# Selective scans in tiles of four states by 32 channels instead of two states by 64, with dt passed on through device memory

## The chip, the core and the metric

The kernel runs on one core of a Trainium2 chip. The metric is the time of one execution on the device, in microseconds (us), as the median of several runs. A profile is one further execution, recorded by the hardware profiler; its span is the time from the first to the last instruction.

The engines: TensorE (PE) multiplies matrices, VectorE (DVE) works elementwise and runs scans, ScalarE (ACT) evaluates functions, GpSimd (POOL) works elementwise, SyncE (SP) issues the DMA transfers. Each executes its own instructions in the order in which they were put into the program; semaphores tie the engines together.

## What is computed

The input is 4 images of 384 channels by 32 x 32 positions, all in fp32. Two layers follow each other, each with a sequence mixer and a feed-forward part. Cut to what matters:

```python
# both mixers: a selective scan over t = 0..1023, 16 states n for each channel d
h[d, n] = h[d, n] * exp(dt[d, t] * A[d, n]) + (dt[d, t] * u[d, t]) * B[n, t]
y[d, t] = sum over n of h[d, n] * C[n, t]

# layer 0: four directions k, 384 channels, each with its own weights
xd = x_proj[k] @ xs[k]                     # rows dt (12), B (16), C (16)
dt = softplus(dt_proj[k] @ xd[:12] + bias)
y  = sum over k of (scan + D * u), turned back; layer norm; gelu
# layer 1: 768 channels, one direction
xin, z = in_proj(x); u = silu(conv4(xin)); scan with dt, B, C from u
out = layernorm(out_proj((y + D * u) * silu(z)))
# after layer 0: a feed-forward of Kronecker weights; after layer 1: 4 experts, best 2
```

## The kernel before

Two functions follow each other: `conv_layers` (L219), which holds all of layer 0 and the mixer of layer 1, and `moe_layer` (L1086), the experts. The change is in the first alone.

**The passes.** A pass (L756 to L778) is one image, one direction or one half of the 768 channels, and one half of the 1024 positions: 384 channels by 512 positions by 16 states. Layer 0 has 8 passes for an image, layer 1 has 4, so there are 48. The order of images and layers is fixed (`order`, L756): layer 1 of an image lies between the layer-0 passes of others.

**The steps.** A pass has 16 steps of three tiles each; a tile is 128 x 512, and its partitions hold two states of 64 channels. A step does:

- `load` (L845): SP fetches the step's B rows (`bt`) and C rows (`ct`) from device memory and broadcasts each to 64 partitions, two transfers for each of the two. Both have rings of three buffers.
- `times_b` (L854): POOL multiplies `dtus` (dt times u) by B for three tiles at once, into a slot of `s`, a ring of five.
- `decay` (L857): ACT computes exp(dt times A) from `dts` into `da`, one PSUM bank for each tile of a step.
- `scan` (L863): DVE runs the recurrence along the 512 positions. A first pass starts from 0, a later one from `state`; `keep_state` (L877) copies the last column.
- `times_c` (L901) and `times_c_pool` (L910): the result times C, by DVE for the first tiles of a step (the scan has then written to `da`) and by POOL for the rest (the scan has written to `s`). `share[i]` says how many DVE takes.
- `add` (L885): PE multiplies each tile by `both`, 128 x 64 of zeros and ones, which sums the two states into 64 partitions of `acc`, three PSUM banks for 384 channels. The tiles of a step go to the halves of PE's columns in turn.
- `gather` (L897, L466, L677): once in a pass, DVE adds `acc` and the D term into the layer's result.

**Ahead of a pass** (`prep_pass`, L374): PE multiplies by the dt weights (L381), ACT adds the bias (L390) and takes softplus (L393, which needs another function table: `exp_set` at L239 loads the old one back), POOL multiplies by u (L397), and SP copies dt and dt times u from SBUF to SBUF into `dts` and `dtus`, which hold each channel once for each of the two states (L409). `prep_quad0` and `prep_quad1` (L436, L645) make the rows of B and C.

**The rest** is side work: layer norms (L312), the feed-forward (`post0`, L482), projection and convolution of layer 1 (`prep1`, L593), gate and output projection (`post1`, L684). It shares all engines with the scans, two PSUM banks (`ps`), three buffers `tmp`, six `t1` and four `w`.

**The order of the work.** A planner (`Plan`, L117) writes out each engine's instructions before anything runs. The steps' instructions are `Op`s (L108) in streams, with a cost and what they depend on; side work is generators (`Lane`, L90), which yield an engine and a cost before each instruction. `run` (L181) takes, over and over, the instruction that can start first by its own clock, and `choose` (L1009) decides between a step's instruction and side work: on ACT side work goes if the next decay is not late by the plan or if it has waited 6 us (`AGE`), on POOL `pool_choice` (L979) does the like, and `split` (L1001) sets `share` by how far POOL is ahead. A DMA counts as 0.1 us on SP in this clock, whatever it is. Side jobs of the images follow each other in one chain (L816): the input of an image's layer 1 is ready only when the chain has reached it. On the chip each engine follows the written order, and waits where something is later than planned.

## Time and profile before

| | |
|---|---|
| median of 3 runs | 6737.26 us (6733.55 to 6745.8) |
| the profiled execution's own time | 6755.91 us |
| its span | 6754.0 us |
| first scan | at 68.86 us |
| last gather of the scans | at 4474 us, then 2.06 us |
| scans stand still | from 4030 to about 4113 us |
| experts | from about 4600 us to the end |
| busy in the span: PE, DVE, ACT, POOL | 5601.9, 4145.4, 2735.4, 4080.2 us |
| mean granted clock of PE | 0.883 |

A line of a group in the profile gives the line of the code, engine and operation, what is written and read, shapes and count; then the busy time in us and the mean of one in ns; then the idle time of the engine just before these instructions, with what ended it. An fp32 matmul of this kernel has two records, so 2304 sums show as 4608. Durations of neighbours overlap a little in the records (two products C of 0.68 us end 1.27 us after the first began), so the pace of an engine is read from start to start. PE's time contains pipelined work and is no measure of its peak. An instruction on a DMA queue (SPq) lasts for as long as it holds the queue; when its data has landed is given apart. Idle time of an engine costs nothing unless another waits for it.

### The profile page before, as it was taken

How to read it: one execution, taken by the hardware profiler on the slowest of the kernel's cores; microseconds unless marked ns; L12 is line 12 of the kernel's file. 1: busy time of each engine (PE TensorE's matmuls, PEld its weight loads, DVE VectorE, ACT ScalarE, POOL GpSimd, SP SyncE). 2: the span in 40 equal slices, each digit the busy share in tenths (PEclk: the TensorE clock that was granted, in tenths of full speed). 3: DMA queues.
4: the chain of work that ended last, by engine and by line, in shares of the span. 5: the costliest groups of instructions: out<-in, count | busy, mean ns of one | idle time of the engine just before them, and what ended most of it. 6: DMA issues, size and time to landing. Idle time of an engine off the chain costs nothing. (4 is left out here: it accounts for less than half of the span.)

```text
span 6754.0 us, 47474 instructions
## 1 busy us (share of the span) xinstructions
PE 5601.9 (83%) x12352; PEld 1929.1 (29%) x12352; DVE 4145.4 (61%) x5421; ACT 2735.4 (41%) x3911; POOL 4080.2 (60%) x1735
## 2 busy tenths in 40 slices
PE   6666789767777876878886897767899999999999
PEld 1111123112122211222221222223444444444444
DVE  6999989998889999899999885951100000000000
ACT  4444565555455645555555554432211111111111
POOL 6999888998889888999899875950000000000000
PEclk8787889887888988888887888888999999999999
DMA  4444444444445444445444433422000000000000
GB/s 130 143 140 143 138 119 141 143 134 124 133 139 159 136 132 139 130 144 157 144 142 138 118 109 106 148 88 105 0 0 0 28 0 8 21 0 0 10 14 14
DMA packets 413489, 644.55 MB, mean 95 GB/s; under 512 B 75104, under 2 KB 119200, under 8 KB 413216
## 3 DMA queue, kind: packets, MB, share of 16 engines
q1 hardware_dynamic: 413216, 641.52, 31.6%
q8 instruction: 97, 1.59, 0.1%
q14 instruction: 176, 1.44, 0.1%
HBM read 468.77 MB, written 21.50 MB: 73 GB/s over the span
## 5 line engine op out<-in xcount | busy, mean ns | idle before, releaser
L855 POOL TENSOR_TENSOR s<-dtus,bt 128x1536 f32<-128x1536 f32 x768 | 2640.6, 3447 | 177.6 <-PE acc L889 94.6
L889 PE MATMUL acc<-s,both 128*64 128x512 f32 x4608 | 2030.3, 742 | 838.1 <-POOL s L913 547.2
L861 ACT ACTIVATE da<-dts,a 128x512 f32<-128x512 f32 x2304 | 1511.2, 683 | 1469.2 <-DVE s L902 1305.7
L1226 POOL TENSOR_TENSOR xb<-xb,yg 128x1536 f32<-128x1536 f32 x32 | 118.8, 3712 | 1834.3 <-DVE yg L1223 1775.4
L1223 DVE SCALAR_TENSOR_TENSOR yg<-py,pvt,gate 128x512 f32<-128x512 f32 x96 | 66.2, 746 | 1848.8 <-PE py L1200 1846.6
L913 POOL TENSOR_TENSOR s<-s,ct 128x512 f32<-128x512 f32 (+1 forms) x673 | 1044.8, 1554 | 207.6 <-DVE state L883 54.4
L889 PEld LDWEIGHTS acc<-s,both 128*64 128x64 f32 x4608 | 483.7, 156 | 2323.9 <-POOL s L913 985.7
L1200 PE MATMUL py<-hid,w 128*128 128x512 f32 x2304 | 1046.2, 592 | 1.5 <-DVE yg L1223 1.5
L1212 PE MATMUL ph<-tb,w 128*128 128x512 f32 x2304 | 1046.3, 592 | 0.0
L870 DVE TENSOR_TENSOR_SCAN da<-da,s 128x512 f32<-128x512 f32 x736 | 871.4, 1219 | 169.3 <-POOL s L855 101.0
L870 DVE TENSOR_TENSOR_SCAN da<-da,state,s 128x512 f32<-128x512 f32 x720 | 889.3, 1273 | 100.0 <-ACT da L861 90.3
L902 DVE TENSOR_TENSOR s<-da,ct 128x512 f32<-128x512 f32 x1456 | 944.0, 682 | 10.9 <-DMA ct<-rows 6.2
L1216 ACT ACTIVATE hid<-ph,pvt 128x512 f32<-128x512 f32 x384 | 263.9, 687 | 1523.2 <-PE ph L1212 1516.9
L1200 PEld LDWEIGHTS py<-hid,w 128*128 128x128 f32 x2304 | 437.7, 190 | 553.9 <-issue 550.4
L1212 PEld LDWEIGHTS ph<-tb,w 128*128 128x128 f32 x2304 | 438.0, 190 | 552.2 <-issue 551.9
L870 DVE TENSOR_TENSOR_SCAN s<-da,state,s 128x512 f32<-128x512 f32 x432 | 550.4, 1274 | 15.8 <-ACT da L861 15.8
L870 DVE TENSOR_TENSOR_SCAN s<-da,s 128x512 f32<-128x512 f32 x416 | 503.8, 1211 | 18.1 <-ACT da L861 17.9
L591 PE MATMUL ps<-u,w 128*128 128x512 f32 x576 | 294.8, 660 | 35.9 <-DMA w<-in_w_in_dram 29.0
L381 PE MATMUL ps<-xd,dtw 12*128 12x512 f32 (+1 forms) x288 | 188.8, 749 | 32.7 <-ACT dt L390 24.5
L543 PE MATMUL ps<-t,w 32*128 32x512 f32 x192 | 148.4, 904 | 40.8 <-DMA w<-in_w_fc_dram 38.6
L591 PEld LDWEIGHTS ps<-u,w 128*128 128x128 f32 x576 | 114.9, 209 | 219.1 <-issue 171.9
L724 PE MATMUL ps<-yx,w 128*128 128x512 f32 x288 | 144.6, 655 | 38.9 <-DMA w<-in_w_out_dram 36.4
(134 smaller groups left out, 3278.1 us busy)
## 6 DMA issues: line engine op xcount, KB each, us to landing
bt<-rows SPq DMA_DIRECT2D x1536, 128.0 KB, 3.0
ct<-rows SPq DMA_DIRECT2D x1536, 128.0 KB, 3.0
dts<-dt SPq DMA_DIRECT2D x192, 256.0 KB, 3.9
dtus<-dt SPq DMA_DIRECT2D x192, 256.0 KB, 3.4
dts<-dt SPq DMA_DIRECT2D x192, 128.0 KB, 3.2
dtus<-dt SPq DMA_DIRECT2D x192, 128.0 KB, 3.5
w<-in_w_dram SPq DMA_DIRECT2D x8, 2304.0 KB, 23.9
w<-in_w_in_dram SPq DMA_DIRECT2D x48, 192.0 KB, 3.0
```

Of the source, the lines that this page charges most:

```text
L381: nc.tensor.matmul(pd, lhsT=q["dtw"][QROW : QROW + nr, c * P : (c + 1) * P], rhs=q["xd"][QROW : QROW + nr, cols(h)], start=True, stop=True,)
L543: nc.tensor.matmul(ph[h], lhsT=w[:32, j, :], rhs=z[h][:32], start=True, stop=True)
L591: nc.tensor.matmul(pi, lhsT=w[:, c, :], rhs=u[:, c, cols(h)], start=c == 0, stop=c == NC - 1)
L855: nc.gpsimd.tensor_tensor(ss[i % NSR], dtus[place(i)[1]], rep(bts[i % NBR]), ALU.mult)
L861: nc.scalar.activation(das[x], dts[part][:, x, :], AF.Exp, scale=q["a"][:, g, m : m + 1])
L870: nc.vector.tensor_tensor_scan(d if in_psum else s, d, s, 0.0 if first else state[:, j, x : x + 1], ALU.mult, ALU.add)
L889: nc.tensor.matmul(acc[side * HP : (side + 1) * HP, c, :], lhsT=both, rhs=ss[i % NSR][:, x, :], start=m == 0, stop=m == NS // 2 - 1,)
L902: nc.vector.tensor_tensor(ss[i % NSR][:, x, :], das[x], cts[i % NCR], ALU.mult)
L913: nc.gpsimd.tensor_tensor(s[:, m:, :], s[:, m:, :], rep(cts[i % NCR], NC - m), ALU.mult)
L1200: nc.tensor.matmul(py[:, m, :], lhsT=w2[:, f, m * P : (m + 1) * P], rhs=hid, start=f == 0, stop=f == NF - 1,)
L1212: nc.tensor.matmul(ph, lhsT=w1[:, c, f * P : (f + 1) * P], rhs=ts[i][:, c, :], start=c == 0, stop=c == NC - 1)
L1216: nc.scalar.activation(hid, ph, AF.Gelu, bias=pv("b1", e * NF + f))
```

## The change

A tile's partitions hold four states of 32 channels instead of two of 64, and a step has four tiles (`NG`) instead of three; a pass has 12 steps, and a chunk of four steps covers 128 channels with all 16 states. Following from it:

- B and C rows are broadcast to 32 partitions each, four transfers for each of `bt` and `ct` in a step.
- POOL's product with B covers four tiles; `share` is 3 by default, and POOL takes none, one or two tiles of a step's product with C.
- `da` has four PSUM banks; the tiles of a step are summed by `four`, 128 x 32, into the four quarters of the partitions of one bank, `acc`. All four sums are one entry of the plan.
- `acc` holds 128 channels, so it is gathered at each chunk's end, 144 times in place of 48, and a chunk's first sum waits for the gather before it.
- dt and dt times u are made in two buffers `tmp`, written to device memory (`spread`), and read from there into `dts` and `dtus`, 128 channels at a time, four transfers for each. These have two buffers in turn of chunks; the next load into one waits for the last decay, or the last product with B, of the chunk two before.
- `s` has four slots of four tiles; `ps` has three banks; `tmp` has four buffers, of which the preparation of a pass claims two.
- The dt weights and projected rows lie in one tile each, in two halves that take turns; layer 1 loads its dt weights once for an image.
- The planner remembers when a buffer was given back (`Free.clock`), and a lane's next instruction isn't planned ahead of that time (`floor`). Its costs and places in a step (`STEP`, `C`, `AT`) are those of steps of four tiles, `SPARE` is 3.6 instead of 6.0, and on PE sums take precedence when they are more than one step behind instead of two.

The diff, cut to its core:

```diff
+        yield "at", at
+        return tile
 
     def give(self, *tiles):
-        self.tiles.extend(tiles)
+        self.tiles.extend((Free.clock, t) for t in tiles)
 
 
...
+        self.floor = now
         try:
             self.want = next(self.gen) if sent is None else self.gen.send(sent)
+            while self.want is not None and self.want[0] == "at":
+                self.floor = max(self.floor, self.want[1])
+                self.want = next(self.gen)
         except StopIteration:
             self.done = True
 
     def ready(self):
-        return self.want[2] if len(self.want) > 2 else self.end
+        return max(self.want[2] if len(self.want) > 2 else self.end, self.floor)
 
 
...
-    dt, dtu = tiles(2, [P, NC, T], "dt")
-    dts = tiles(2, [P, NC, T], "dts")
-    dtus = tiles(2, [P, NC, T], "dtus")
-    xds = tiles(2, [64, L], "xd")
-    dtws = tiles(2, [64, D], "dtw")
+    NG, NJ = 4, 4 * NC
+    dts = tiles(2, [P, NG, T], "dts")
+    dtus = tiles(2, [P, NG, T], "dtus")
+    xd = sp.tile([P, L], F32, name="xd")
+    dtw = sp.tile([P, 2 * D], F32, name="dtw")
     wxs = tiles(2, [P, NC, QROW + R0], "wx")
-    NSR, NBR, NCR = 5, 3, 3
-    ss = tiles(NSR, [P, NC, T], "s")
+    NSR, NBR, NCR = 4, 3, 3
+    ss = tiles(NSR, [P, NG, T], "s")
     bts = tiles(NBR, [P, T], "bt")
     cts = tiles(NCR, [P, T], "ct")
-    state = sp.tile([P, NS, NC], F32, name="state")
-    tmp = Free(tiles(3, [P, NC, T], "tmp"))
+    state = sp.tile([P, NJ, NG], F32, name="state")
+    tmp = Free(tiles(4, [P, NC, T], "tmp"))
     t1 = Free(tiles(6, [P, T], "t1"))
     wts = Free(tiles(4, [P, NC, P], "w"))
-    acc = ps_1.tile([P, NC, T], F32, name="acc")
-    das = tiles(NC, [P, T], "da", pool=ps_1)
-    ps = Free(tiles(2, [P, T], "ps", pool=ps_1))
+    acc = ps_1.tile([P, T], F32, name="acc")
+    das = tiles(NG, [P, T], "da", pool=ps_1)
+    ps = Free(tiles(3, [P, T], "ps", pool=ps_1))
...
     nc.vector.tensor_tensor(spread, spread, proj2[:32, :D], ALU.mult)
 
 
-    both = wp.tile([P, HP], F32, name="both")
-    nc.vector.tensor_tensor(both, ident[:, :HP], ident[:, HP:], ALU.add)
-    a0 = wp.tile([P, 8 * NC, NS // 2], F32, name="a0")
-    a1 = wp.tile([P, 2 * NI, NS // 2], F32, name="a1")
+    four = wp.tile([P, QP], F32, name="four")
+    nc.vector.tensor_tensor(four, ident[:, :QP], ident[:, QP : 2 * QP], ALU.add)
+    for k in (2, 3):
+        nc.vector.tensor_tensor(four, four, ident[:, k * QP : (k + 1) * QP], ALU.add)
+    a0 = wp.tile([P, 4 * NC * NG, NS // 4], F32, name="a0")
...
     def prep_pass(q, p, h, u, u_view):
 
 
...
+        spread = dram.tile([2, D, T], F32, tag="dts", name="dts", bufs=3)
+        dt = yield from tmp.take(True)
+        dtu = yield from tmp.take(True)
         for c in range(NC):
             pd = yield from ps.take(True)
             yield PE, 0.95
             nc.tensor.matmul(
                 pd,
-                lhsT=q["dtw"][QROW : QROW + nr, c * P : (c + 1) * P],
-                rhs=q["xd"][QROW : QROW + nr, cols(h)],
+                lhsT=dtw[dt_rows(q), q["w0"] + c * P : q["w0"] + (c + 1) * P],
+                rhs=xd[dt_rows(q), cols(h)],
                 start=True,
                 stop=True,
             )
...
         yield ACT, 1.45 + SWITCH
         nc.scalar.activation(dt, dt, AF.Softplus)
         exp_set()
+        yield SP, LOAD
+        nc.sync.dma_start(out=spread[0].rearrange("(c p) t -> p c t", p=P), in_=dt)
         for c in range(NC):
             yield POOL, 1.35
             nc.gpsimd.tensor_tensor(u_view(dtu[:, c, :]), u_view(dt[:, c, :]), u[:, c], ALU.mult)
-        for part in range(2):
-            before = 0.0
-            if p:
-                before = yield from until(("scan", NS * (p - 1) + 8 * part + 7, 2))
-            for to, of in ((dts[part], dt), (dtus[part], dtu)):
-                yield SP, LOAD, before
-                for side in range(2):
-                    mine = [x for x in range(NC) if (3 * part + x) % 2 == side]
-                    chunks = [(3 * part + x) // 2 for x in mine]
-                    for k in range(2):
-                        nc.sync.dma_start(
-                            out=to[k * HP : (k + 1) * HP, mine[0] : mine[-1] + 1 : 2, :],
-                            in_=of[side * HP : (side + 1) * HP, chunks[0] : chunks[-1] + 1, :],
-                        )
-            plan.end["pass", p, part] = plan.now + LOAD + 2.0
+        tmp.give(dt)
+        yield SP, LOAD
+        nc.sync.dma_start(out=spread[1].rearrange("(c p) t -> p c t", p=P), in_=dtu)
+        tmp.give(dtu)
+        for part in range(NC):
+            n = NC * p + part
+            i = 4 * (n - 2) + 3
+            for k, (to, last) in enumerate(((dts[n % 2], ("da", i, NG - 1)), (dtus[n % 2], ("b", i)))):
+                before = 0.0
+                if n >= 2:
+                    before = yield from until(last)
+                of = spread[k, part * P : (part + 1) * P].rearrange("(q r) t -> r q t", r=QP)
+                for i4 in range(4):
+                    yield SP, LOAD, before
+                    nc.sync.dma_start(out=to[i4 * QP : (i4 + 1) * QP], in_=of)
+            plan.end["pass", p, part] = plan.now + LOAD + 1.0
...
-    def gather1(b, g, h):
+    def gather1(b, g, h, c):
         xc = st[("xc", b)][g]
-        for j in range(NC):
-            nc.vector.scalar_tensor_tensor(
-                xc[:, j, cols(h)], xc[:, j, cols(h)], pv("d1", g * NC + j, 1), acc[:, j, :], ALU.mult, ALU.add
-            )
+        nc.vector.scalar_tensor_tensor(
+            xc[:, c, cols(h)], xc[:, c, cols(h)], pv("d1", g * NC + c, 1), acc, ALU.mult, ALU.add
+        )
 
...
+        return i // 4
 
     def load(i, of, ring):
-        p, part, m = place(i)
-        for k in range(2):
-            row = of + 2 * m + k
+        p, c, m = place(i)
+        rows = quad(p)["rows"]
+        for k in range(4):
+            row = of + 4 * m + k
             nc.sync.dma_start(
-                out=ring[i % len(ring)][k * HP : (k + 1) * HP, :],
-                in_=quad(p)["rows"][row : row + 1, cols(passes[p][4])].partition_broadcast(HP),
+                out=ring[i % len(ring)][k * QP : (k + 1) * QP, :],
+                in_=rows[row : row + 1, cols(passes[p][4])].partition_broadcast(QP),
             )
 
     def times_b(i):
-        nc.gpsimd.tensor_tensor(ss[i % NSR], dtus[place(i)[1]], rep(bts[i % NBR]), ALU.mult)
+        nc.gpsimd.tensor_tensor(ss[i % NSR], dtus[part_of(i) % 2], rep(bts[i % NBR], NG), ALU.mult)
 
     def decay(i, x):
-        p, part, m = place(i)
+        p, c, m = place(i)
         q = quad(p)
-        g = 2 * q["c0"] + 3 * part + x
-        nc.scalar.activation(das[x], dts[part][:, x, :], AF.Exp, scale=q["a"][:, g, m : m + 1])
+        g = NG * (q["c0"] + c) + x
+        nc.scalar.activation(das[x], dts[part_of(i) % 2][:, x, :], AF.Exp, scale=q["a"][:, g, m : m + 1])
 
     def scan(i, x):
...
-    def add(i, xs):
-        _, part, m = place(i)
-        for x in xs:
-            c, side = divmod(3 * part + x, 2)
+    def add(i):
+        _, c, m = place(i)
+        for x in range(NG):
             nc.tensor.matmul(
-                acc[side * HP : (side + 1) * HP, c, :],
-                lhsT=both,
-                rhs=ss[i % NSR][:, x, :],
-                start=m == 0,
-                stop=m == NS // 2 - 1,
+                acc[x * QP : (x + 1) * QP, :], lhsT=four, rhs=ss[i % NSR][:, x, :], start=m == 0, stop=m == 3
             )
 
-    def gather(p):
+    def gather(p, c):
         _, layer, b, k, h, _, _ = passes[p]
-        (gather0 if layer == 0 else gather1)(b, k, h)
+        (gather0 if layer == 0 else gather1)(b, k, h, c)
+        if c == NC - 1:
+            plan.end["gather", p] = plan.end["gather", p, c]
 
...
-    STEP, C1, SPARE = 4.8, 1.24, 6.0
-    share = dict.fromkeys(range(N), 2)
-    main, gathers, decays, bs, cs, bl, cl = ([] for _ in range(7))
-    adds = [[], []]
-    AT = (0.0, 1.18, 3.6)
+    STEP, C1, SPARE = 6.6, 1.24, 3.6
+    C = (0.0, 3.42, 2.35, C1, 0.0)
+    share = dict.fromkeys(range(N), 3)
+    main, gathers, decays, bs, cs, bl, cl, adds = ([] for _ in range(8))
+    AT = {"scan": (0.0, 1.18, 3.6, 4.78), "mult": (2.36, 2.98, 5.96, STEP), "state": (2.36, 5.96)}
...
-        bs.append(Op(("b", i), 3.42, [("pass", p, part), ("bt", i), *ring], lambda i=i: times_b(i)))
-        for x in range(NC):
+        bs.append(Op(("b", i), 4.6, [("pass", p, part), ("bt", i), *ring], lambda i=i: times_b(i)))
+        for x in range(NG):
             free = [("da free", i - 1, x)] if i else []
             decays.append(Op(("da", i, x), 0.63, [("pass", p, part), *free], lambda i=i, x=x: decay(i, x)))
...
+        for what, x in (
+            ("scan", 0), ("scan", 1), ("state", 0), ("mult", 0), ("mult", 1),
+            ("scan", 2), ("scan", 3), ("state", 1), ("mult", 2), ("mult", 3),
...
-        wait = [("gather", p - 1)] if m == 0 and p else []
-        for k, xs in enumerate(((0, 1), (2,))):
-            adds[k].append(
-                Op(("add", i, k), 0.95, [("part", i, x) for x in xs] + wait, lambda i=i, xs=xs: add(i, xs))
-            )
-        if i % NS == NS - 1:
-            gathers.append(
-                Op(("gather", p), 2.0, [("add", n, k) for n in (i - 8, i) for k in range(2)], lambda p=p: gather(p))
-            )
+        wait = [("gather", (i // 4 - 1) // NC, (i // 4 - 1) % NC)] if m == 0 and i else []
+        adds.append(Op(("add", i), 1.0, [("part", i, x) for x in range(NG)] + wait, lambda i=i: add(i)))
+        if m == 3:
+            cost = 1.1 if passes[p][1] == 0 and passes[p][3] % 2 else 0.75
+            gathers.append(Op(("gather", p, part), cost, [("add", i)], lambda p=p, c=part: gather(p, c)))
...
-            return NC
-        return 1 if ahead - waiting > SPARE else 2
+            return NG
+        return 2 if ahead - waiting > SPARE else 3
 
```

## The prediction

> **What bounds the kernel now.** I read the page from the top, then the busy time by stretch, the waits, and the queue of SP.
>
> ```profile
> 150.00:4000.00 3850.00, 2967.73 (x6286) 819.83 (x6288) 3546.40 (x4597) 2078.96 (x2993) 3490.38 (x1471) 0.84 0.46 138
> 4000.00:4090.00 90.00, 86.65 (x206) 31.23 (x202) 31.94 (x35) 44.17 (x66) 23.06 (x11) 1.00 0.10 33
> 4090.00:4480.00 390.00, 271.72 (x572) 79.66 (x573) 332.13 (x441) 181.40 (x257) 326.81 (x146) 0.82 0.46 137
> ```
>
> Columns: stretch, length, then busy us of PE, PE weight load, DVE, ACT, POOL, then clock, DMA share, GB/s. The scans run from 69 to 4476 us. In the long stretch DVE is busy 92% and POOL 91%; PE has 77%. From 4030 to 4113 the scans stand still: the last image's layer-1 input is not ready, and PE alone works. After 4480 comes the mixture of experts, bound by PE, which the change leaves alone.
>
> ```profile
> DVE da L870 <- ACT da L861: 158.3, 99, 6.0
> DVE da L870 <- POOL s L855: 104.1, 9, 82.5
> DVE s L870 <- ACT da L861: 33.7, 18, 4.3
> POOL s L855 <- PE acc L889: 94.6, 50, 7.0
> ```
>
> (us, times, longest.) In its scans DVE waits 192 us for a decay from ACT, and 104 us for POOL, of which 82.5 is the standstill. So DVE's own work is the bound, and the largest thing on top of it is ACT coming late. Why it comes late shows at 2647 us:
>
> ```profile
> 2647.21 1.28 ACT L495 ACT_TABLE_LOAD   x1
> 2648.51 2.23 ACT L495 ACTIVATE yx<-yx,pvt 128x512 f32<-128x512 f32 x3
> 2650.75 1.28 ACT L239 ACT_TABLE_LOAD   x1
> 2652.84 2.35 DVE L870 TENSOR_TENSOR_SCAN da<-da,s 128x512 f32<-128x512 f32 x2 [1.89 <-ACT da L861]
> ```
>
> A side job with two table loads holds ACT for 4.8 us; the next decays stand behind it, and DVE idles 1.89 us. The costs of the parts:
>
> ```profile
> L855 POOL TENSOR_TENSOR s<-dtus,bt 128x1536 f32<-128x1536 f32 x768 | 2640.6, 3447 | 177.6 <-PE acc L889 94.6 <-issue 35.5 <-DMA dtus<-dt 16.5
> L902 DVE TENSOR_TENSOR s<-da,ct 128x512 f32<-128x512 f32 x1456 | 944.0, 682 | 10.9 <-DMA ct<-rows 6.2 <-issue 1.1 <-PE ps L543 0.7
> L913 POOL TENSOR_TENSOR s<-s,ct 128x512 f32<-128x512 f32 x498 | 633.8, 1273 | 140.1 <-issue 36.5 <-DVE state L883 29.4 <-DVE s L870 25.6
> L913 POOL TENSOR_TENSOR s<-s,ct 128x1024 f32<-128x1024 f32 x175 | 411.0, 2353 | 67.6 <-DVE state L883 24.9 <-DVE s L870 19.7 <-issue 12.2
> ```
>
> POOL's price rises by 1.08 to 1.09 us for each 512 columns (1.273, 2.353, 3.447), with some 0.19 fixed. Then PE's sums, and SP's queue (min/median/max ns of one issue):
>
> ```profile
> 4030.07 1.93 PE L889 MATMUL acc<-s,both 128*64 128x512 f32 x6
> L849 SPq DMA_DIRECT2D bt<-rows x1536: 444/587/1947, 42.3 to 4450.4; - x192
> L409 SPq DMA_DIRECT2D dts<-dt x384: 477/621/1527, 56.3 to 4395.2; - x192
> SPq L849 <- POOL s L855: 1122.1, 538, 9.4
> ```
>
> Three tiles (six records) take 1.93 us where they run back to back. SP spends about 0.59 us on each transfer whatever its size (a 12-partition one takes 0.40), and has 1122 us in which it only waits for a buffer.
>
> **What the Trainium skill says.** "TensorE: Matmul & The Clock Gate", Part 3 (packing small matmuls): matmuls whose outputs lie in different column groups run at the same time; it has 2.38 times for three column tiles. The trace agrees for halves: tiles go to halves 0, 1, 0, and 1.93 us is two rounds of 0.96. No row shows four quarters. "Perfetto Trace Analysis", DMA Instruction — HWDGE: a DMA's duration on its queue is the descriptor work, not the movement. The trace agrees: 0.59 us on SP, landing after 3.0. "DMA: Bandwidth & Descriptors", Anatomy of one DMA: the fixed part is mostly the receipt of the write, heaviest for device memory (told there of another queue). The trace agrees in kind: rows written to memory land after 4.0 us, 128 KB into SBUF after 3.0.
>
> **The change, part by part.** The counts are from the two programs' instruction orders.
>
> *Shape of a step.* 768 steps of three tiles become 576 of four; 2304 tiles, scans and decays stay. POOL, B products: 768 x 3.447 = 2641; four tiles should take 3.447 + 1.09 = 4.54, and 576 x 4.54 = 2615: -26. POOL, C products: 498 x 1.273 + 175 x 2.353 = 1046 become 350 x 2.353 + 128 x 1.273 = 986: -59. POOL loses 85 us, but the path gets only what DVE waits for POOL outside the standstill, about 104 - 82 = 22 us: I take -15 (0 to -22). DVE gets 20 more C products (1476): back to back two take 1.19, so 20 x 0.6 = +12, all on the path.
>
> *ACT's slack.* Before, a step is 4.72 us; the first decay's buffer is free after scan, scan, product (3.0 us), the decay takes 0.69, and it is needed at 4.72: 1.0 us to spare, and ACT's hole in a step is 2.25 us (the gap before the decays in steady steps). A side block above 3.3 us makes DVE wait. Blocks with two table loads: 48 softplus of 4.0 us (0.7 too long), 8 of 4.8 (1.5), and 40 of 5.4 (2.1; 1.28 + 2.86 + 1.28): 34 + 12 + 84 = 130 of the 192 us. After, a step is 4 x 1.18 + 3 x 0.6 = 6.5 us, free at 3.0, needed at 6.5: 2.8 to spare, limit 5.1 us; only the 40 are too long, by 0.3: 12 us. That is -118. The rest of the 192 is ACT standing behind a side copy that waits for PE (109 us at L546 alone, waits that need not reach DVE). I take -105 (-20 to -150).
>
> *Sums.* 768 x 1.93 = 1482 us of PE become, if four quarters share a round, 576 x about 1.0 (one round of 0.96 and a little) = 576. PE is not the bound, so this is cover: DVE waits for PE in layer norms and feed-forward about 36 us in the long stretch; -15 (-36 to 0). If quarters don't overlap, 576 x 3.9 = 2250, see the rivals.
>
> *acc in one bank, gathered per chunk.* 144 gathers instead of 48. Work: 24 plain ones of 0.68 against 8 of 1.75 (+2), 48 turned of about 1.06 against 16 of 2.98 (+3): +5. New wait: the first sum of a chunk waits for the gather, and side matmuls on PE stand behind it; POOL waits behind that for a slot of s (94.6 us today). The ring of s is 16 tiles instead of 15, so it hides about as much, 4 x 6.5 = 26 us. DVE waits for sums before gathers 50 us today (29 of it layer 1). +20 (-30 to +90).
>
> *dt over memory.* Per pass two writes of 768 KB and 24 reads instead of 16 copies. Hidden by the lead: softplus stands 26 tiles (42 us) ahead of its pass in ACT's order (39, 63 us, before), and the way is about 20 us: product 4, write 4.0, eight issues 5, landing 3.5. Where nothing covers it, at the start and in the standstill, it adds about 4 us of write and 1.1 of the larger product: +5 each. SP waits there for the write to land, with loads of B and C behind it.
>
> *The standstill.* PE's order has 68 side tiles between the last sum before it and the first after it, then 49: 16 convolution tiles less (four take 3.7 us): -15; with the +5, -10. At the start +5.
>
> *SP.* B and C loads go from 3072 to 4608, of half the size; dt from 768 to 1152. For one chunk (144 of them): 32 x 0.585 + 8 x 0.62 + 0.3 (writes) + 1.3 (about 330 other loads) = 25.3 us. A chunk will take (4476 - 69 - 83 - 90) / 144 = 29.4 us. So SP goes from about 55% to 86%. The loads still have two steps (13 us) of lead, and need 2.3 issue, 3 landing and up to 5 behind a dt burst. +15 (0 to +200).
>
> *Other PSUM, weights, tmp:* a third ps buffer, one load of the layer-1 dt weights for two, four tmp of which dt takes two for about 20 us of a pass, the planner's later claims: these lie beside the scans; zero, and if the cover goes they are in the range of ACT's term.
>
> **Sum** against the profiled execution: -15 + 12 - 105 - 15 + 5 + 20 - 10 + 5 + 15 = -88. Its span 6754.0 becomes 6666; its own time of 6755.91 lies 18.7 above the median of 6737.26, so I subtract from the median: 6649. With ACT's and SP's bounds alone this case runs from 6600 to 6724.
>
> **Rivals.** (1) *SP becomes the bound*: slower. It decides where a chunk's issues exceed 29.4 us, that is where SP's prices are 1.16 times today's (0.68 us for a load). For it: the maximum is already 1.9 us, dt reads come from memory, DMA bytes rise by about a fifth. Against it: most issues lie at 0.45 to 0.59, and half-size loads may be cheaper. At 1.23 times, 31.1 us, 144 x 1.7 = +245, less the 45 that SP's wait then hides of other waits: 6850. (2) *Quarters don't overlap*: PE gets 770 us more on 77% busy, and everything aside comes late; at 4400 us of scans PE would be over 95%: 6880. Against it: halves do overlap. (3) *No change*: ACT's lateness comes from PE and weight loads rather than from its own blocks, and SP, fuller, brings weights later; -105 shrinks to -20, the rest cancels: 6735. (4) *All stalls go*: 192 + 36 + 22 with 17 of added DVE work, -10 and +5: 6737 - 238 = 6500; for it, DVE would be at 97%, and POOL has 85 us less.
>
> **Chances.** Forecast 6649: 0.59. Rival 1: 0.16. Rival 2: 0.05. Rival 3: 0.09. Rival 4: 0.11. A measurement tells 0.2% (13 us) from no change. Faster: forecast and rival 4, 0.70; within: rival 3, 0.09; slower: rivals 1 and 2, 0.21. The range takes in rival 4 and most of rival 1 below its point: 6500 to 6830.
>
> **What would show it.** Right: DVE's waits for decays fall from 192 below 90 us; eight records of the sums take about 1.0 us; B products take 4.5 us; the long stretch shows DVE at 94% or more; DVE's and POOL's waits for bt, ct, dts, dtus stay below 40 us. Wrong: SP's queue without waits for POOL and DVE or POOL waiting for loads (rival 1); sums of 3.9 us a step (rival 2); gathers that wait over 90 us.

## The result, and the profile after

The changed kernel takes 6822.38 us (median of 4 runs, 6820.19 to 6824.42) against 6739.12 us of the kernel before beside it: the ratio is 1.0123, with a 95% interval of 1.0106 to 1.0141. It is 83 us slower; the forecast was 88 us faster. The profiled execution took 6824.42 us with a span of 6822.6, so 68.6 us more than the span shown before. The experts' part is the same (2277.8 us from the last gather to the end before, 2275.7 after); the last gather ends at 4546.9 instead of 4476.2 us.

Four stretches of the scans hold these 71 us. The first scan comes 14.5 us later (83.34 for 68.86). The way from there to the standstill takes about 47 us more. The standstill is about 15 us shorter. The last stretch, from its end to the last gather, takes 24 us more. (The prediction and the section on the kernel before give 4113 for the end of the standstill; the trace has the scans resume at 4125.5. Of the prediction only SP's time for a chunk uses it, which becomes 29.3 us instead of 29.4.)

Busy times by stretch after the change, in the columns of the prediction's first view:

```profile
150.00:4000.00 3850.00, 2462.61 (x6183) 586.07 (x6183) 3498.00 (x4624) 2051.19 (x2951) 3363.56 (x1110) 0.71 0.67 165
4000.00:4090.00 90.00, 86.11 (x264) 31.01 (x263) 83.70 (x93) 55.77 (x98) 76.38 (x24) 0.96 0.48 119
4090.00:4480.00 390.00, 226.21 (x540) 60.91 (x538) 267.20 (x374) 172.92 (x235) 271.47 (x100) 0.71 0.59 147
```

In the long stretch DVE is busy 90.9% instead of 92.1%, and POOL 87% instead of 91%: both engines that were near their limit now wait more. The last two columns are the new thing: the DMA engines' share of the time went from 0.46 to 0.67, while the bytes moved rose only from 138 to 165 GB/s. The waits of DVE (us, times, longest):

```profile
DVE da L888 <- POOL s L873: 176.4, 29, 77.7
...
DVE da L888 <- ACT da L879: 59.8, 33, 9.0
DVE yx L700 <- PE acc L907: 49.8, 16, 11.2
DVE yx L494 <- PE acc L907: 46.5, 10, 10.7
...
DVE s L888 <- ACT da L879: 39.0, 14, 7.3
...
DVE yx L501 <- PE acc L907: 36.4, 12, 7.7
```

The waits for decays are 98.8 us instead of 192: that part came nearly as forecast. But DVE waits 176.4 us for POOL's B products (104.1 before; 77.7 of it is the standstill), and its gathers wait for PE's sums (L494, L501, L700; with 11.9 us at L498 it is 145 us). The costs of single operations came as forecast too:

```profile
L873 POOL TENSOR_TENSOR s<-dtus,bt 128x2048 f32<-128x2048 f32 x576 | 2605.5, 4532 | 304.1 <-DMA bt<-rows 80.4 <-DMA dtus<-dts 76.3 <-issue 56.7
...
L918 DVE TENSOR_TENSOR s<-da,ct 128x512 f32<-128x512 f32 x1476 | 952.4, 682 | 41.6 <-DMA ct<-rows 30.5 <-PE acc L907 4.0 <-issue 1.1
...
L929 POOL TENSOR_TENSOR s<-s,ct 128x1024 f32<-128x1024 f32 x350 | 824.5, 2356 | 114.8 <-DVE s L888 44.0 <-DVE state L901 40.7 <-DMA ct<-rows 11.2
...
L929 POOL TENSOR_TENSOR s<-s,ct 128x512 f32<-128x512 f32 x128 | 162.9, 1273 | 117.7 <-issue 63.0 <-DVE state L901 19.5 <-DMA ct<-rows 16.2
```

The B product takes 4.53 us (forecast 4.54). What has changed is behind the second bar: its idle time ahead is 304.1 us instead of 177.6, and ends on transfers, where before it ended on PE. SP's issues, by the view of its line (min/median/max ns) and then its waits:

```profile
L867 SPq DMA_DIRECT2D bt<-rows x2304: 302/419/1870, 44.9 to 4515.4; - x192
```

```profile
SPq L867 <- DMA dtus<-dts: 438.0, 525, 2.2
SPq L867 <- POOL s L873: 429.9, 197, 8.7
```

A load of half the size is issued in 0.419 us instead of 0.587, so SP spends no more time on issues than before (2050 us of the 3650 between 100 and 3750 us, against 2005). But it now stands 438 us for dt's own transfers, 0.83 us at a time.

The trace shows what it stands for. The program's transfers take eight semaphores in turn, and an issue waits until the transfer eight before it, which had the same semaphore, has landed; none of the 6128 issues is an exception. So no more than eight transfers are under way. Eight reads of dt fill all eight places, and of these a read into `dts` lands 5.1 us after its issue at the median, one into `dtus` 7.2 us (3.5 and 3.6 us in the kernel before). What stands behind such a burst in SP's order, B and C rows and weights, goes out one by one as the reads land. Between 100 and 3750 us SP waits 686 us for landings in this way, and 5 us in the kernel before.

**A pass that starts late.** Pass 12 shows the new wait for POOL whole. ACT has finished its softplus at 1103.2 us. SP, POOL and DVE (start, duration, then the instruction; in brackets the idle time ahead of it):

```profile
1103.22 0.38 SPq L417 DMA_DIRECT2D dts<-tmp  x1
...
1135.58 0.38 SPq L423 DMA_DIRECT2D dts<-tmp  x1
1136.06 2.56 SPq L435 DMA_DIRECT2D dts<-dts  x4
1140.29 1.73 SPq L435 DMA_DIRECT2D dtus<-dts  x4
```

```profile
1119.68 1.28 POOL L420 TENSOR_TENSOR tmp<-tmp,u 128x512 f32<-128x512 f32 x1
...
1126.64 1.27 POOL L420 TENSOR_TENSOR tmp<-tmp,u 128x512 f32<-128x512 f32 x1
...
1133.71 1.27 POOL L420 TENSOR_TENSOR tmp<-tmp,u 128x512 f32<-128x512 f32 x1
1134.94 1.28 POOL L929 TENSOR_TENSOR s<-s,ct 128x512 f32<-128x512 f32 x1
1149.60 8.96 POOL L873 TENSOR_TENSOR s<-dtus,bt 128x2048 f32<-128x2048 f32 x2 [13.38 <-PE acc L907]
```

```profile
1154.12 2.35 DVE L888 TENSOR_TENSOR_SCAN da<-da,s 128x512 f32<-128x512 f32 x2 [12.09 <-POOL s L873]
```

POOL's three products of dt and u stand one in each step of its order, so the last ends 32 us after softplus. Only then can the second write go out, and the reads of `dtus` wait until it has landed. The last of the eight reads, issued at 1141.6, has landed at 1149.4, 7.8 us later. In the 14 us from 1136 the DMA engines are full (busy share 1.04 by the view), where it was 0.31 in the 15 us from 1120: the mean of 0.67 is made of such bursts and of quiet stretches. POOL has nothing else for 13.4 us, and DVE idles 12.1. (The row names PE as the releaser, but the sum of the step that held the slot was over at 1124.2. Of the passes that start late, ten have POOL standing for a transfer, the first pass and the one after the standstill left out. In all ten the B product begins 0.1 to 0.4 us after the last read of `dtus` has landed, and that landing takes 5.6 to 8.2 us, as here.)

**A gather that waits.** At 3172 us an output projection on PE has got its weights late:

```profile
3162.58 1.37 SPq L435 DMA_DIRECT2D dts<-dts  x3
3164.04 1.30 SPq L435 DMA_DIRECT2D dtus<-dts  x1
3165.43 0.39 SPq L367 DMA_DIRECT2D w<-in_w_out_dram  x1
3165.87 1.43 SPq L435 DMA_DIRECT2D dtus<-dts  x3
```

```profile
3172.08 5.49 PE L744 MATMUL ps<-yx,w 128*128 128x512 f32 x6 [4.73 <-DMA w<-in_w_out_dram]
3177.50 1.13 PE L907 MATMUL acc<-s,four 128*32 128x512 f32 x8
```

```profile
3178.78 0.75 DVE L494 SCALAR_TENSOR_TENSOR yx<-u,dsum,acc 128x512 f32<-128x512 f32 x1 [6.63 <-PE acc L907]
```

The weights were issued in the middle of a burst of dt and landed 6.6 us later; PE stood for them; the chunk's last sums stood behind; DVE idled 6.63 us. Of the 30 gathers that wait over 1 us, 25, with 122 of 136 us, have their last sums start right behind a side block on PE, and in 17 of these (98 us) the block had itself stood for a load. The eight records of a step take 1.13 us: four quarters do run at once.

### The profile page after: what moved, and what is told of

The parts are those of the page before. It is cut to its first block, busy times and chain, and to the rows that moved or that the text cites. A ratio compares the mean times of both kernels' runs of the same rounds, so it can differ in the third digit from the quotient of the medians.

```text
span 6822.6 us, 49036 instructions
## 1 busy us (share of the span) xinstructions
PE 5064.4 (74%) x12352; PEld 1681.2 (25%) x12352; DVE 4137.3 (61%) x5491; ACT 2731.8 (40%) x3911; POOL 3998.3 (59%) x1348
## 3 DMA queue, kind: packets, MB, share of 16 engines
q1 hardware_dynamic: 506768, 767.48, 44.7%
## 5 line engine op out<-in xcount | busy, mean ns | idle before, releaser
L873 POOL TENSOR_TENSOR s<-dtus,bt 128x2048 f32<-128x2048 f32 x576 | 2605.5, 4532 | 304.1 <-DMA bt<-rows 80.4
L907 PE MATMUL acc<-s,four 128*32 128x512 f32 x4608 | 1430.4, 840 | 1208.7 <-POOL s L929 739.0
L929 POOL TENSOR_TENSOR s<-s,ct 128x1024 f32<-128x1024 f32 (+1 forms) x478 | 987.4, 2066 | 232.4 <-issue 71.0
L888 DVE TENSOR_TENSOR_SCAN da<-da,state,s 128x512 f32<-128x512 f32 x738 | 911.6, 1276 | 57.1 <-ACT da L879 36.1
L907 PEld LDWEIGHTS acc<-s,four 128*32 128x32 f32 x4608 | 203.8, 126 | 2369.0 <-POOL s L929 1112.0
L888 DVE TENSOR_TENSOR_SCAN s<-da,state,s 128x512 f32<-128x512 f32 x414 | 510.9, 1268 | 13.1 <-ACT da L879 13.1
L888 DVE TENSOR_TENSOR_SCAN s<-da,s 128x512 f32<-128x512 f32 x414 | 486.1, 1205 | 26.1 <-ACT da L879 25.9
L744 PE MATMUL ps<-yx,w 128*128 128x512 f32 x288 | 171.5, 751 | 102.4 <-DMA w<-in_w_out_dram 99.8
L564 PE MATMUL ps<-t,w 32*128 32x512 f32 x192 | 162.9, 998 | 96.9 <-DMA w<-in_w_fc_dram 95.2
L402 PE MATMUL ps<-xd,dtw 12*128 12x512 f32 (+1 forms) x288 | 203.4, 816 | 17.3 <-ACT tmp L411 12.8
```

Source lines behind the costliest of these rows:

```text
L402: nc.tensor.matmul(pd, lhsT=dtw[dt_rows(q), q["w0"] + c * P : q["w0"] + (c + 1) * P], rhs=xd[dt_rows(q), cols(h)], start=True, stop=True,)
L744: nc.tensor.matmul(po, lhsT=w[i][:, c, :], rhs=xc[i][:, c, cols(h)], start=i + c == 0, stop=i * NC + c == NI - 1,)
L873: nc.gpsimd.tensor_tensor(ss[i % NSR], dtus[part_of(i) % 2], rep(bts[i % NBR], NG), ALU.mult)
L888: nc.vector.tensor_tensor_scan(d if in_psum else s, d, s, 0.0 if first else state[:, j, x : x + 1], ALU.mult, ALU.add)
L907: nc.tensor.matmul(acc[x * QP : (x + 1) * QP, :], lhsT=four, rhs=ss[i % NSR][:, x, :], start=m == 0, stop=m == 3)
L929: nc.gpsimd.tensor_tensor(s[:, m:, :], s[:, m:, :], rep(cts[i % NCR], NG - m), ALU.mult)
```

## The experiments

Two theories stand at first. **Theory 1**: the transfers of dt over memory come late or make others late; in 1a by their bytes, in 1b by their number, in 1c because reading from memory is slow, in 1d because eight of 256 KB stand in a row in SP's queue; later 1e, because dtus is the last of the eight, and 1f, because a pass's dt is made with too little lead. **Theory 2**: the sums of a chunk in one PSUM bank, gathered 144 times, hold up DVE. Each run stands beside runs of the kernel before, whose median lay between 6741 and 6748 us. Three edits (dt_quarter, bc_one, before_more) leave the written order of every engine as it was. The others pass through the planner, which then writes the orders of all engines anew; what that alone is worth was not measured.

**A quarter of dt's bytes (dt_quarter).** Three quarters of the bytes that are read back are left out.

```diff
+w = NG if n < 2 else 1
-nc.sync.dma_start(out=to[i4 * QP : (i4 + 1) * QP], in_=of)
+nc.sync.dma_start(out=to[i4 * QP : (i4 + 1) * QP, :w], in_=of[:, :w])
```

> The changed kernel, but each of the 1152 transfers that bring dt and dt times u back from memory carries one of its four groups after the first two chunks, so three quarters of those bytes are left out (302 MB become 76; the scans then run on old values there). Number, order and issue of the transfers stay. Theory 1a (the bytes that dt moves make all loads land late): the DMA share of the scans falls from 0.67 to about 0.48, POOL's waits for bt, ct, dtus fall from 190 to below 70 us, PE's waits for weights from 255 to about 100, and the time is 6750 us. Theory 1b (the number of transfers does it): share above 0.6, time 6805. Theory 2 (the gathers and the sums that stand in order on PE): gathers still wait over 90 us, time 6810 to 6822.

6531.72 us, 291 us below the changed kernel. All waits shrink: DVE's for gathers from 103 to 34 us and for decays from 74 to 36 (100 to 3750 us), though nothing about the gathers, and no engine's order, was changed. PE's waits for weights (`w` and `wx`, whole run) fall from 342 to 139 us, and SP's for landings from 686 to 23. Theory 2 loses its ground, and theory 1 is right in kind at four times the size that I had given it.

**One transfer instead of four for B, and for C (bc_one).**

```diff
-for k in range(4): ...  # one row to 32 partitions each
+nc.sync.dma_start(out=ring[i % len(ring)], in_=rows[row : row + 4, ...].unsqueeze(1).to_broadcast([4, QP, T]))
```

> The changed kernel, but the four B rows of a step come by one transfer of 256 KB instead of four of 64 KB, and the C rows likewise: the same bytes, 1152 transfers in place of 4608. Theory 1b (the number of transfers): the DMA share falls from 0.67 to about 0.5, waits for loads are at least halved, time 6750 us. Theory 1a (the bytes): share and time as in the changed kernel, 6822. Theory 2: 6810 to 6822 with gathers still waiting over 90 us.

7574.22 us, 752 us slower. The DMA share does fall (page: 37.1% of the span on the queue, 44.7% in the changed kernel), and still everything comes later. The waits of DVE in this run:

```profile
DVE s L915 <- DMA ct<-rows: 519.3, 136, 9.5
```

So the mean share of busy DMA engines doesn't tell when a transfer lands. In the trace the semaphore of a load of this form is counted up five times as it lands, where that of a load of the changed kernel is counted up sixteen times, and in five loads that stood alone at most six packets were under way at once (14 to 19 there). So only some of the DMA engines carry such a load; its C rows land after 11.6 us at the median instead of 2.1. The number of transfers is thus not all that this run changes, and theory 1b gets nothing from it.

**Two banks for the sums (two_acc), then a later gather besides (late_gather).**

```diff
-acc[x * QP : (x + 1) * QP, :]
+accs[part_of(i) % 2][x * QP : (x + 1) * QP, :]     # ps: 2 banks instead of 3
```

```diff
-Op(("gather", p, part), cost, [("add", i)], ...)
+Op(("gather", p, part), cost, [("add", i), ("scan", i + 1, NG - 1)], ...)
```

> The changed kernel, but chunks take their sums in two PSUM banks in turn, and side work has two banks instead of three: the first sum of a chunk no longer waits for the gather of the one before. Theory 2: PE's waits for gathers (72 us) go, DVE's waits for sums fall from 110 to about 70 us, time 6770. Theory 1: the gathers wait for sums that are late for other reasons, time 6815 to 6830.

> As the run with two banks, and the gather of a chunk is put into DVE's order one step later, behind the last scan of the next step (within a pass). Theory 2: DVE's waits for sums fall from 110 to below 30 us, time 6735 to 6750. Theory 1: these waits fall too, but POOL's waits for loads (190 us) then come to stand on the path, time 6790 to 6822.

6836.00 and 6853.44 us: both slower. PE's waits for gathers, 93 us in the changed kernel, are gone in both, and yet the gathers wait 106 and 112 us, as before (103). The bank that side work loses may cost something in its turn. Theory 2 falls: a bank more is no help where the last sum itself is late.

**B and C kept for a pass (bc_keep).** Rings of four, and loads only for the first chunk of a pass; for room, t1 has four buffers.

```diff
+if part == 0:
     bl.append(Op(("bt", i), ...)); cl.append(Op(("ct", i), ...))
```

> The changed kernel, but the four groups of B and C rows stay in SBUF for a pass (rings of four), so that they are loaded once in a pass and not three times: 1536 transfers in place of 4608, 201 MB less; the dt traffic is as in the changed kernel. Side work has four t1 buffers instead of six. Theory 1a (the load on the DMA engines as a whole): DMA share of the scans from 0.67 to about 0.45 and nearly the gain of the run with a quarter of dt's bytes: 6560 us, DVE's waits for sums below 60 us. Theory 1c (the lateness of dt's own transfers): the waits for dtus and dts stay at about 130 us, 6750. Theory 2: 6800.

6731.65 us: 201 MB and 3072 transfers less gain 91 us, but 17 of 48 passes still begin late, and gathers still wait 102 us. Load on the DMA engines is worth as much as the whole slowdown, and yet taking it off leaves both of these waits as they were.

**dt in pairs, dtus first (dt_spread).**

```diff
-for k, (to, last) in enumerate(((dts..., ("da", i, NG - 1)), (dtus..., ("b", i)))):
+for k, to in ((1, dtus[n % 2]), (0, dts[n % 2])):
     for i4 in range(4):
+        on = i + i4 // 2
+        before = yield from until(("b", on) if k else ("da", on, NG - 1))
```

> The changed kernel, but the eight transfers of a chunk's dt go out in four pairs, dtus after the B products of two successive steps and dts after their decays, instead of eight in a row after the last decay; bytes and number are the same. Theory 1d (the burst of 2 MB stands ahead of B, C and weights): waits for weights fall from 255 to about 120 us, 6700. Theory 1a (the mean load): 6800 to 6822, with the waits spread over more places.

6653.68 us: 169 us gained with every byte and every transfer in place, and 1.4% faster than the kernel before (0.9863, 0.9846 to 0.9879). DVE's waits for POOL's B go from 64 to 1 us and for gathers from 103 to 37. Theory 1a, in which the mean load does it, falls.

**The kernel before with more traffic (before_more), and with dt over memory (before_mem).**

```diff
+nc.sync.dma_start(out=more[n_more, :, : len(mine)], in_=src)   # beside each copy of dt
```

> The kernel before, and beside each of its 768 copies of dt a second one of the same size into device memory that nobody reads: 151 MB more, 768 transfers more, nothing else. Theory 1a: this is the changed kernel's traffic without its other parts; DMA share from 0.46 to about 0.6, time 6800 to 6850. Theory 2 or a cause in the steps' shape: 6740 to 6760.

```diff
+nc.sync.dma_start(out=over[0]..., in_=dt)                      # and over[1] from dt times u
-in_=of[side * HP : (side + 1) * HP, chunks...]                 # SBUF
+in_=over[j]...[side][:, chunks...]                             # device memory
```

> The kernel before, with dt and dt times u written to device memory and its 768 copies read from there; shape of steps, sums and gathers as before. It is the way over memory alone: 75 MB of writes more, the copies' bytes the same. Theory 1a: about +20 us, 6760. Theory 1c (reading dt back from memory is what is slow): 6800 or more.

7261.54 us, a loss of 515 us where some 60 to 110 were expected, and 6713.21 us, a gain (0.9947, 0.9932 to 0.9962). The first was no clean test of bytes: its bursts of sixteen hold SP 14.0 us at the median, longer than the two steps (9.4 us) that the rings of B and C reach, and DVE waits 277 us for C (100 to 3750 us; 6 in the kernel before). The second is clear: with the steps and the lead of the kernel before, going over memory costs nothing as such, which ends theory 1c. That it gains 34 us I can't explain; its copies are issued in 0.61 us on average instead of 0.73, and its orders are written anew.

**Order alone (dt_early), pairs alone (dt_pairs), another queue (dt_act_queue).**

```diff
-enumerate(((dts[n % 2], ("da", i, NG - 1)), (dtus[n % 2], ("b", i))))
+((1, dtus[n % 2], ("b", i)), (0, dts[n % 2], ("da", i, NG - 1)))
```

> The changed kernel, with the order of a chunk's dt transfers changed alone: the four of dtus first, allowed after the last B product that reads the old ones, then the four of dts after the last decay as now. Bursts of eight become mostly bursts of four. Theory 1d (a burst stands ahead of B, C and weights): about half of what the spreading gained (169 us), 6740. Theory 1e (dtus came too late, being last): nearly all of it, 6660. Theory 1a: 6810.

```diff
+on = (i, NG - 1) if e < 2 else (i + 1, 1) if e < 4 else (i + 1, NG - 1) if e < 6 else (i + 2, 1)
+before = yield from until(("da", *on))        # order as in the changed kernel
```

> The changed kernel, with a chunk's dt transfers in the present order but in pairs, each two decays later than the one before: bursts of two, and dtus arrives one to two steps later than now. Theory 1d: waits for weights and C fall as with the spreading, POOL's waits for dtus stay about as they are, 6680 to 6740. Theory 1e: dtus is later still, 6850 or more.

```diff
-yield SP, LOAD, before
-nc.sync.dma_start(out=to[i4 * QP : (i4 + 1) * QP], in_=of)
+yield ACT, 0.1, before
+nc.scalar.dma_start(out=to[i4 * QP : (i4 + 1) * QP], in_=of)
```

> The changed kernel, with the 1152 transfers that read dt back issued by ACT instead of SP, in the same bursts of eight; loads of B, C and weights stay with SP. Theory 1d in the form that the burst holds up what is queued behind it on SP's own queue: SP's waits for dts and dtus (650 us) and the waits for weights go, and the time falls, less what 3.4 us of issuing for a chunk costs ACT: 6650 to 6720. If the burst fills the DMA engines for everybody: waits for bt and weights stay, 6810 to 6880.

6679.45, 6822.75 and 7788.60 us. The order alone gains 143 of the 169 us, and a read into `dtus` lands after 4.1 us at the median instead of 7.2. Pairs alone gain nothing on balance, a result between the two expectations: DVE's waits for B go up from 64 to 170 us, since dtus is issued later still, while its other waits fall from 254 to 174. So it matters most when dtus lands (theory 1e), which POOL, the engine furthest ahead, needs first; shorter bursts help too, but less (26 us between this order and the pairs with dtus first). The third run shows what the wait for landings does to the engine that issues:

```profile
2000.87 4.01 ACTq L435 DMA_DIRECT2D dts<-dts  x2
2004.97 6.92 ACTq L435 DMA_DIRECT2D dtus<-dts  x4
```

Each of these six issues lasts 0.31 to 0.39 us. In the rest of the 10.9 us ACT waits, before four of them, until a transfer that had the same semaphore has landed, here always a load of B or C that SP had issued. Its decays stand behind (DVE waits 869 us for them). SP and ACT share the eight semaphores, so the run says nothing on whose queue is better for the loads.

**Both together (keep_and_spread).**

> The changed kernel with both: B and C rows kept for a pass (four t1 buffers), and dt's transfers spread in pairs with dtus first. Theory 1d: what keeping B and C gained (90 us) overlaps with the spreading (169 us), since both take away loads that meet a burst: 6590 to 6640. If the gains are of different kinds they add: 6560.

The edits of bc_keep and dt_spread. 6588.28 us: 234 of the 259 us that they gain singly.

**The lead of a pass's dt.** The transfers of dt can wait in the order without harm if they are there in time, so lead was tried by itself: longer in the changed kernel (prep_early), and shorter in the kernel before (before_late).

```diff
+plan.end["made", p] = plan.now                  # after the second write
-deps = [...] + ([("pass", p - 1)] if p else [])
+deps = [...] + ([("made", p - 1)] if p else [])
```

> The changed kernel, but the preparation of a pass may begin once the one before it has written its dt to memory, not only when all of that one's loads are in the order: its softplus stands 72 to 120 decays ahead of its pass instead of 26. Transfers, bytes, their order and the bursts of eight stay. Theory 1f (the lead of a pass's dt was too short: POOL's first B product of a pass waits for it): no pass begins with POOL waiting for dtus, DVE's waits for POOL (64 us) and for sums (110 us) fall to about 10 and 40, time 6680 or less. Theory 1d (bursts): 6800.

```diff
-deps = [...] + ([("pass", p - 1)] if p else [])
+deps = [...] + ([("pass", p - 1), ("scan", NS * (p - 1) + 3, 2)] if p else [])    # kernel before
```

> The kernel before, with the preparation of a pass held back to the fourth step of the pass ahead of it, so that softplus stands about 26 decays ahead of its pass, as in the changed kernel, instead of 39. Nothing else is changed. Theory 1f: its copies of dt have some 27 us to spare between the eighth issue and the first B product, and lose 21, so part of the passes start late: 6760 to 6830. Theory 1d, and all in which the shape of the steps or the traffic does it: 6740.

6660.95 us (0.9883, 0.9864 to 0.9901): 161 us gained, with bursts of eight, dtus last, and all bytes. POOL and DVE at the start of pass 12 in that run:

```profile
1106.11 4.53 POOL L874 TENSOR_TENSOR s<-dtus,bt 128x2048 f32<-128x2048 f32 x1
```

```profile
1108.16 2.32 DVE L889 TENSOR_TENSOR_SCAN da<-da,s 128x512 f32<-128x512 f32 x2
```

No idle time ahead of either. POOL's idle time before the first B product of a pass, the standstill left out, sums to 5 us in the kernel before, 133 in the changed one, and 19 here, 18 of them ahead of the first pass (gaps over 1 us). But the gathers still wait 93 us (103), and SP still waits 655 us for landings: this edit takes away what a late landing cost at the start of a pass, and not the late landing.

before_late is a miss: 6721.86 us, no slower than the kernel before (0.9973, 0.9966 to 0.9981). So a short lead alone does no harm there. Medians over the passes (the first and the one after the standstill left out), in us from the end of softplus, show why:

| | product with u done | eighth transfer issued | first B product | first scan |
|---|---|---|---|---|
| before | 8.7 | 32.6 | 59.7 | 67.8 |
| before_late | 8.3 | 12.4 | 38.1 | 46.6 |
| changed | 20.5 | 28.8 | 40.6 | 49.3 |
| prep_early | 17.6 | 144.9 | 164.5 | 173.1 |

With the same lead as the changed kernel, before_late has 25.7 us between the eighth issue and the B product that needs it; the changed kernel has 11.8, of which landing takes some 7. The change shortened the lead by 18 us and lengthened the way as well; neither alone did harm in the kernel before (here, and in the run with dt over memory).

**All together.** Early preparation with the new order and B and C kept (prep_keep_order), with pairs besides (prep_keep_spread), and without keeping B and C (prep_spread).

> The changed kernel with the early preparation, dtus ahead of dts, and B and C rows kept for a pass (four t1 buffers). Theory 1f: the order and the lead answer the same lateness, so this lies near the run that keeps B and C and spreads dt (6588): 6540 to 6600.

> As the run before it, with dt in pairs besides. Theory 1f: within 15 us of that run; theory 1d: faster by 30 us or more.

> The changed kernel with the early preparation and with dt's transfers in pairs, dtus first; B and C rows are loaded as in the changed kernel, six t1 buffers. If the short lead at a pass's start and the burst ahead of the weights are two causes, each worth some 160 us alone, they add for the most part: 6540 to 6580. If they are one and the same lateness: 6640 to 6660, as with either alone.

6509.54, 6482.40 and 6524.65 us, the first 31 and the last 15 us faster than their expected ranges. The last settles the count of causes: early preparation and the new order with pairs gain 298 us together, of 161 and 169 singly. They are two, and nearly add. Pairs beyond the order bring 27 us here, between what the two theories allowed. SP's waits for landings (100 to 3750 us) are 218 us in the last run and 30 in the second; but singly this sum does not set the time, for it is 655 us in prep_early, 600 in dt_early, 498 in dt_spread, and 429 in dt_pairs, which gained nothing. The version with all three, at 6482.40 us, is 3.8% faster than the kernel before (0.9618, 0.9604 to 0.9632).

DVE's waits between 100 and 3750 us, summed by what it waited for, put the runs side by side:

| | decays | B products | sums, for a gather | loads of B and C | side work and rest | sum | time |
|---|---|---|---|---|---|---|---|
| before | 162 | 11 | 27 | 13 | 42 | 255 | 6739 |
| changed | 74 | 64 | 103 | 28 | 49 | 318 | 6822 |
| prep_early | 48 | 3 | 93 | 14 | 53 | 211 | 6661 |
| dt_early | 106 | 0 | 36 | 40 | 30 | 213 | 6679 |
| dt_spread | 109 | 1 | 37 | 15 | 36 | 199 | 6654 |
| prep_spread | 26 | 0 | 40 | 1 | 28 | 95 | 6525 |
| prep_keep_spread | 25 | 0 | 21 | 0 | 27 | 72 | 6482 |

## Why the prediction was wrong

**What held.** POOL's prices and counts, DVE's 20 further C products, the sums at about 1.1 us a step, the experts untouched. *ACT's slack*: DVE's waits for decays fell by 93 us (105 forecast), to 98.8 where I had named 90 as the sign. In prep_spread, where little else is late, 26 of 162 us are left in the window of the table, which fits the reasoning on side blocks; its size was, if anything, low. *The standstill* is 15 us shorter (10 forecast). The 15 us that a freer PE was to bring did not come: DVE waits 22 us for the matmuls of layer norms before and 23 after, in the table's window.

**What failed first: "Hidden by the lead".** The step said that softplus stands 42 us ahead, the way is about 20 us, "product 4, write 4.0, eight issues 5, landing 3.5" (which add up to 16.5), and the rest is cover; it took +5 each at the start and in the standstill. The lead was there, 49.3 us from the end of softplus to the first scan. The way was not. The product takes 20.5 us, since POOL's order puts its pieces between the products of three steps, and it took 8.7 already in the kernel before. From the first read to the last landing it is 13.3 us in pass 12, not 8.5. And I counted the lead to the scan, where it ends at POOL's B product, 8.7 us earlier (49.3 - 40.6). 17 of 48 passes begin with a B product that ends as the scan starts (within 0.35 us). In the ten of them in which POOL had stood for a transfer, the product is done after 25 us, the eighth read is issued after 34 and the B product begins after 41, at the median: the way is as long as the lead, and nothing is left. An earlier preparation alone gains 161 us. The same error at the start: forecast +5, measured 14.5, of which SP's second write, issued at 64.44 us instead of right behind the product (60.9), is 3.5.

**What failed second: the gathers, "+20".** They wait 76 us more than before (103 and 27, in the table's window). The reason that I gave, that one bank must be free before the next sums, is not the one: two banks changed nothing. The gathers wait because the last sums stand on PE behind side matmuls whose weights came late: waits for the three kinds of weights are 286 us on PE (99.8, 95.2, 91.0) instead of 104 (36.4, 38.6, 29.0). The range for this term, to +90, did hold it, and rival 3 had named later weights, though only as what would keep ACT late. Gathers that wait over 90 us stood among the signs of being wrong, and came.

**What failed third: SP, "+15".** Its price was mis-sized in one direction (0.419 us a load, not 0.585) and its meaning in the other. The term counted the time of issues and put the wait for an earlier landing at nothing; it is 686 us. Rival 1 gave 6850, near the time by luck: its issues were to take 1.16 times as long and more, and they got shorter, and SP still waits 430 us for POOL to free buffers. What grew is the time until a transfer has landed. The Trainium skill, "Perfetto Trace Analysis", DMA Instruction — HWDGE, has the movement of data outside the time reported for a DMA instruction; I used that section to price issues and then took 3 us of landing from a trace with fewer bytes in flight. The eight reads of a burst of 2 MB land 5.5 to 7.8 us after their issues in pass 12. (A smaller slip: 768 x 3.447 is 2647 us, not 2641; it lies off the path.)

What is shown: two causes, each removed alone and together (prep_early, dt_early or dt_spread, prep_spread). That the loss comes from late transfers, and not from newly written orders, is shown by the run with a quarter of dt's bytes: at unchanged orders it gains 291 us, about as much as the two together. In it the gathers that wait over 1 us fall from 136 to 35 us, and those behind a side block that had stood for a load from 98 to 10; so late weights do hold up the gathers. What stays open is how dtus's place in the queue spares them. In dt_early PE still waits 303 us for weights (342 in the changed kernel, `wx` included), but its gathers only 66 us by the same count, of which 25 us stand behind a block that waited for a load: the lateness meets fewer last sums, and the order on PE is another one there.

## What to carry to other kernels

When a transfer is put on a path that was hidden, lay out the path step by step in the trace, with each step's place in its engine's order and not its duration, and end it at the engine that runs furthest ahead and not at the one that sets the time. Among transfers that go out together, the one that the furthest engine needs comes first: in the run that changed this order alone it was worth 2%. Where an issue waits for the landing of an earlier transfer, count how many may be under way and how long each takes to land, and not only how long an issue lasts: large transfers in a row then hold back the small ones behind them. A wait that names an engine as its releaser may be two steps downstream of a late load; leaving out part of the bytes showed in one run how much hung on it.

## What was not expected of the hardware

- Packets of 2 KB take 84 ns at the median in the kernel before, 121 in the changed one, and 81 at the fifth percentile in both; with a quarter of dt's bytes the median is 84 again.
- Under bursts of eight the time to land doubles: 7.2 us at the median for a read into `dtus`, the last of the eight, against 3.6 for the copies of the kernel before, and 4.1 where dtus goes first. An issue itself doesn't last longer (0.43 us on SP, 0.31 on ACT).
- A broadcast of four rows to 128 partitions in one transfer, instead of four of one row to 32, made the kernel 752 us slower, at a lower DMA share; the trace has five updates of its semaphore for such a load and not sixteen.
- PE's granted clock in the long stretch fell from 0.84 to 0.71 with PE busy 64% instead of 77%. It is either 1.0 or 0.5 in the records, and at 0.5 for 2239 of the 3850 us instead of 1266. So a higher busy share isn't what lowers it here. PE's idle gaps over 3 us went from 61 to 154, which goes with it and is no proof. Nor does the lower clock explain the lost time: prep_spread has 0.74 and is 298 us faster.
